# Layer 2 of a graph network with experts: both scores in one table row, experts' work rationed by columns, smaller last batches

## The chip, the cores and the metric

The kernel runs on one core of a Trainium2 chip. The metric is the device time of one execution in microseconds. Several executions are made, and the median counts. In the profile PE is TensorE (PEld are its weight loads), DVE is VectorE, ACT is ScalarE, POOL is GpSimd and SP is SyncE, which here only issues DMAs.

## The reference

The input has 6250 nodes of 256 features and 206,250 directed edges (src, dst). All is float32.

```python
def _gat_layer(x, src, dst, W, b, a, g, beta, N, concat):
    h = x @ W.T + b
    s_src, s_dst = h @ a[:d], h @ a[d:]
    e = jnp.exp(-leaky_relu(s_src[src] + s_dst[dst], 0.2))
    h_prime = segment_sum(e[:, None] * h[dst], src, num_segments=N)
    h_prime = (h_prime - mean) * rsqrt(var + 1e-5) * g + beta
    return elu(h_prime) if concat else h_prime
# layer 1: 8 heads of 64 features on layernorm(x), concatenated to 512
# layer 2: one head, 512 -> 256, elu;  x = x + that
# experts: t = layernorm(x); the 2 best of 8 by softmax(t @ router.T), weights normed to 1
#   y = t + sum over e of weight[e] * (gelu(t @ w1[e] + b1[e]) @ w2[e] + b2[e]);  x = x + y
```

## The kernel before

Nodes are cut into 49 blocks of 128 (the last has 106). One launch goes through three stages.

**The sort** (to about 440 us). The edges are sorted by the block of their src into slots of DRAM, on all engines. Beside it the table of layer 1 is made block by block: `products` (L357) multiplies the turned block by the weights, 512 features and 2x8 scores, `table_rows` (L366) copies them out of PSUM and stores a row of 520 numbers a node in `tab1`. `ph` is the bank of the features, `pk` that of the scores.

**Layer 1 and layer 2** are both run by `edges` (L587). A block has 34 tiles of 128 edges (the last 30), a group is up to 5 tiles (`GT`), so a block has 7 groups and a layer 342. A group goes through seven stages: `sources` loads the edges' places in the block (`rb`, SP); `gather` (L645) fetches the table row of each edge's dst, one indirect DMA a tile on POOL; `one_hot` (DVE) and `source_sums` (PE, `ps`) bring the src scores to the edges; `weigh` (DVE) adds the dst score from the row and ScalarE takes the Exp; `messages` (DVE) makes the weighted one-hot matrix `hot`; `add` (PE, L700) sums the messages into the block's PSUM bank `acc`. The order is written out by hand: a loop of ticks, in each of which every stage works on a group so many ticks ahead:

```python
stages = [(weigh, 2), (messages, 1), (source_sums, 4), (add, 0), (one_hot, 5), (sources, 5 + RB), (gather, GB)]
```

In layer 2 `GB` is 8, and there are as many gather buffers. Engines work in order, each through its own queue. A few "far" edges are added to every block at its end (`far_hot`).

When a block's last group is added, its `block_done` is put into `running`. It is a generator that is advanced once a tick, after the stages. In layer 1 (`middle`) it norms the block and multiplies it by layer 2's weights, and stores 257 numbers a node (256 features and the dst score) in `tab2` (L845), and the src score, one number a node, in `ssrc2` (L847). Layer 2 starts its gathers when the whole table is there.

In layer 2 (`tail`, L852) `block_done` (L902) norms the block, adds it to x (`xq`), norms again (`tok`), turns it on PE, multiplies by the router (`pl`) and, with the last block of a batch of `BB` = 4, finds the two best experts (`routes`). Then the batch's `experts` (L995) is put into `todo`, again a generator. Its steps are: `combine` (turn the weights, `pc`), 16 of `inner` (a half of one expert's first product for the whole batch, `ph`, L1019, then Gelu on ScalarE), `biases`, and 16 of `outer` (one expert's second product for two blocks, `py`, L1027, then two additions into `xq` on DVE, L1032). What takes a step's result off PSUM is issued two steps behind. After each tick `more` (L1069) issues steps:

```python
if steps is None:
    state["credit"] = min(state["credit"] + 1.5, 2.0)
    steps = int(state["credit"])
    state["credit"] -= steps
```

So a tick issues one or two steps, and after the last group all that is left is issued. There are 13 batches: twelve of four blocks and one of the last block alone. Where the sort's tables would overflow, another path through all edges (`every_edge`) is there; it is not taken with these inputs.

Of the kernel before, what the change touches and what calls it, by code (L numbers as in the profile page):

```python
# [31 lines left out]
P = 128  # L32
# [16 lines left out]
def kernel(ctx: ExitStack, tc: tile.TileContext, x, src, dst, w_heads, b_heads, a_heads,  # L49
# [8 lines left out]
    R2 = F + 1  # L58
# [34 lines left out]
    ssrc2 = dram.tile([NB * P, 1], F32, name="ssrc2")  # L93
# [263 lines left out]
    def products(b):  # L357
        ph = bank("ph", "ph")
        pk = bank("pk", "pk")
        for to, cols in ((ph, slice(0, HD)), (pk[:, :2 * H], slice(HD, C1))):  # L360
            for k in range(KF):
                nc.tensor.matmul(to, blocks[b][:, k, :], wt[:, k, cols], start=(k == 0), stop=False)
            nc.tensor.matmul(to, three, bias3[:, cols], start=False, stop=True)
        blocks[b] = ph, pk

    def table_rows(b):  # L366
        ph, pk = blocks.pop(b)
        row = sw.tile([P, C1], F32, name="row", bufs=2)
        nc.scalar.copy(row[:, HD:], pk[:, :2 * H])
        nc.scalar.copy(row[:, :HD], ph)  # L370
# [216 lines left out]
    def edges(es, layer, table, sel, ssrc, k, width, block_done, more=None):  # L587
# [3 lines left out]
        row = width + k  # L591
# [7 lines left out]
        groups = [(b, g) for b in range(NB) for g in range(-(-tiles[b] // GT))]  # L599
# [7 lines left out]
        def where(n):  # L607
            b, g = groups[n]
            return b, b // RBL, (b % RBL) * PITCH + g * GT

        def size(n):
            b, g = groups[n]
            return min(GT, tiles[b] - g * GT)
# [4 lines left out]
        def far_messages():  # L618
# [4 lines left out]
            ss = eb.tile([P, k], F32, name="far_ss")  # L623
            nc.gpsimd.indirect_dma_start(out=ss, out_offset=None, in_=ssrc,
# [7 lines left out]
            nc.vector.tensor_add(ss, ss, far_gt[:, width:])  # L632
# [6 lines left out]
        def sources(n):  # L639
            b, g = groups[n]  # L640
            r0 = b * PIT + g * GT * P
# [23 lines left out]
        def weigh(n):  # L665
# [4 lines left out]
            nc.vector.tensor_add(ssum, ssum, now[n]["gt"][:, :nt, width:])  # L670
# [6 lines left out]
        def messages(n):  # L677
# [17 lines left out]
            if n + 1 == len(groups) or groups[n + 1][0] > b:  # L695
# [4 lines left out]
        def add(n):  # L700
            b, g = groups[n]
# [11 lines left out]
        stages = [(weigh, 2), (messages, 1), (source_sums, 4), (add, 0), (one_hot, 5), (sources, 5 + RB), (gather, GB)]  # L713
        running = []
        t = -5 - RB
        with tc.manual_schedule():
# [5 lines left out]
            while t < len(groups) or running or (more and more(len(groups))):  # L722
# [9 lines left out]
                for of in list(running):  # L732
                    if of[0] <= t and next(of[1], True):
                        running.remove(of)
                if more and t < len(groups):
                    more()
                t += 1

    def every_edge(es, layer, table, ssrc, k, width):

        row = width + k
# [14 lines left out]
        with tc.For_i(0, EC, 1) as i:  # L756
# [7 lines left out]
            sg = gw.tile([EP, k], F32, name="sg")  # L764
            nc.gpsimd.indirect_dma_start(out=sg, out_offset=None, in_=ssrc,
                                         in_offset=bass.IndirectOffsetOnAxis(ap=si, axis=0))
            nc.vector.tensor_add(sg, sg, gt[:, width:])
# [34 lines left out]
    def middle(ms):  # L802
        mw = ms.enter_context(tc.tile_pool(name="mid_w", bufs=2))

        def block_done(b, acc):
# [39 lines left out]
            nc.sync.dma_start(tab2[b * P:(b + 1) * P, :], row[:, :R2])  # L845
# [315 lines left out]
```

## Time and profile before

| | |
|---|---|
| median of three executions | 5668.95 us (5641.82 to 5675.06) |
| profiled execution | 5686.65 us, span 5684.9, mean granted clock of TensorE 0.834 |
| busy | PE 4175.9 (73%), DVE 3288.7 (58%), POOL 3390.8 (60%), ACT 1309.7 (23%) |
| gathers L649 | 3324 on POOL, 965 ns each |

| stretch, us | PE busy | DVE busy | POOL busy | granted clock |
|---|---|---|---|---|
| 0 to 440, sort | 343.3 | 376.4 | 182.0 | 0.90 |
| 440 to 3110, layer 1 | 1944.0 | 1722.8 | 1596.9 | 0.82 |
| 3200 to 3450, layer 2, mostly without experts | 128.6 | 103.3 | 168.9 | 0.72 |
| 4000 to 4600, layer 2 with experts | 462.4 | 290.6 | 396.5 | 0.85 |
| 5585 to 5685, the end | 83.0 | 34.9 | 0.0 | 0.89 |

The views are read like this. The page's slices give each engine's busy share in 40 equal parts. A table of stretches gives busy time (and the number of instructions) of each engine between two moments. A row of the waits says who waited, for whom, how long in total, how often, and the longest. "issue" is idle time that no wait in the profile explains, "remote" one whose releaser is not told. The chain of waits goes back from the last instruction, at each step to what released it. A product in float32 appears as two rows of PE.

### The profile page before, as it was taken

How to read it: one execution, taken by the hardware profiler on the slowest of the kernel's cores; microseconds unless marked ns; L12 is line 12 of the kernel's file. 1: busy time of each engine (PE TensorE's matmuls, PEld its weight loads, DVE VectorE, ACT ScalarE, POOL GpSimd, SP SyncE). 2: the span in 40 equal slices, each digit the busy share in tenths (PEclk: the TensorE clock that was granted, in tenths of full speed). 3: DMA queues.
4: the chain of work that ended last, by engine and by line, in shares of the span. 5: the costliest groups of instructions: out<-in, count | busy, mean ns of one | idle time of the engine just before them, and what ended most of it. 6: DMA issues, size and time to landing. Idle time of an engine off the chain costs nothing.

```text
span 5684.9 us, 52631 instructions
## 1 busy us (share of the span) xinstructions
PE 4175.9 (73%) x16462; PEld 2477.2 (44%) x16462; DVE 3288.7 (58%) x8048; ACT 1309.7 (23%) x2440; POOL 3390.8 (60%) x3450
## 2 busy tenths in 40 slices
PE   5984777777777777777776447777778777777778
PEld 4762333333333333333333335555555555545556
DVE  9975666666666666666666334454444445444444
ACT  1220111111111111111111113333334333333433
POOL 3446656665666666666554666666666666666660
PEclk8996878888888888888778668888888888888989
DMA  2216767786677777777665544444444444444440
GB/s 69 66 51 186 196 187 188 195 210 182 195 192 186 201 190 194 190 195 191 184 189 141 141 118 111 122 119 113 119 122 112 121 120 120 113 119 122 112 112 14
DMA packets 378008, 825.33 MB, mean 145 GB/s; under 512 B 91759, under 2 KB 210779, under 8 KB 377718
## 3 DMA queue, kind: packets, MB, share of 16 engines
q0 software_dynamic: 216464, 665.03, 44.0%
q1 hardware_dynamic: 155868, 151.02, 9.5%
q10 hardware_dynamic: 5386, 5.83, 0.3%
q8 instruction: 131, 2.15, 0.2%
q14 instruction: 159, 1.30, 0.1%
HBM read 792.59 MB, written 28.99 MB: 145 GB/s over the span
## 4 chain that ended last, share of the span: by engine, by line
PE 35%; DVE 26%; issue 17%; another core or an unknown queue 12%; POOL 7%; DMA 2%; DVEq 0%; ACT 0%; POOLq 0%; ACTq 0%; SPq 0%
PE acc L705 18%; DVE msg L687 10%; POOL gt L649 7%; PE ph L1019 6%; PE py L1027 6%; DVE hot L684 2%; DMA gt<-tab,dst_idx 2%; DVE hot L693 1%; DVE ot L656 1%; PE run_ps L278 1%; PE ps L662 1%; DVE ssum L670 1%; DVE ssum L668 1%; DVE what L266 1%
## 5 line engine op out<-in xcount | busy, mean ns | idle before, releaser
L649 POOL DMA_INDIRECT gt<-tab,dst_idx x3324 | 3206.4, 965 | 1908.4 <-issue 923.3
L705 PE MATMUL acc<-msg,hot 128*128 128x512 f32 x3324 | 1711.6, 659 | 180.4 <-issue 178.6
L705 PE MATMUL acc<-gt,hot 128*128 128x256 f32 x3324 | 1004.0, 445 | 176.2 <-issue 167.8
L705 PEld LDWEIGHTS acc<-msg,hot 128*128 128x128 f32 x3324 | 666.4, 209 | 944.5 <-issue 942.9
L687 DVE TENSOR_TENSOR msg<-gt,ee 128x2560 f32<-128x2560 f32 (+1 forms) x342 | 935.2, 2735 | 0.0
L705 PEld LDWEIGHTS acc<-gt,hot 128*128 128x128 f32 x3324 | 697.7, 219 | 337.1 <-issue 230.5
L585 ACT ACTIVATE ee<-lr 128x40 f32<-128x40 f32 (+3 forms) x684 | 141.7, 207 | 2348.7 <-DVE lr L584 1250.0
L662 PE MATMUL ps<-sel,ot 128*128 128x24 bf16 (+1 forms) x3324 | 204.4, 171 | 649.7 <-issue 314.8
L693 DVE TENSOR_SCALAR hot<-iota_n,sloc,ee 128x128 f32<-128x128 f32 x1662 | 461.6, 357 | 330.9 <-remote 166.6
L684 DVE TENSOR_TENSOR hot<-iota_ps,sloc 128x640 f32<-128x640 f32 (+1 forms) x342 | 273.4, 799 | 603.8 <-remote 514.2
L662 PEld LDWEIGHTS <-ot 128*128 128x128 bf16 x3324 | 192.3, 100 | 945.5 <-issue 707.0
L1032 DVE SCALAR_TENSOR_TENSOR xq<-py,comb,xq 128x256 f32<-128x256 f32 x392 | 171.0, 478 | 577.2 <-remote 162.5
L1027 PE MATMUL py<-w2s,h 128*128 128x256 f32 x1568 | 410.5, 402 | 57.9 <-issue 52.9
L1019 PE MATMUL ph<-tokt,w1s 128*128 128x512 f32 (+1 forms) x832 | 408.0, 618 | 25.1 <-issue 23.6
L585 ACT ACT_TABLE_LOAD x252 | 323.3, 1283 | 375.8 <-DVE lr L584 178.6
L1027 PEld LDWEIGHTS py<-w2s,h 128*128 128x128 f32 x1568 | 312.2, 203 | 149.9 <-issue 99.9
L283 POOL DMA_INDIRECT srt<-run,to x92 | 168.4, 1830 | 247.9 <-DMA srt<-run,to 148.8
L668 DVE TENSOR_REDUCE ssum<-ps 128x40 f32<-128x120 f32 (+3 forms) x684 | 149.6, 219 | 252.8 <-remote 197.4
L656 DVE TENSOR_SCALAR ot<-rb,iota_p 128x640 bf16<-128x640 bf16 (+1 forms) x684 | 259.0, 379 | 7.2 <-DMA rb<-srow 7.2
L1019 PEld LDWEIGHTS ph<-tokt,w1s 128*128 128x128 f32 x832 | 162.4, 206 | 168.1 <-issue 157.9
L1021 ACT ACTIVATE h<-ph,b1s 128x512 f32<-128x512 f32 (+1 forms) x208 | 135.5, 662 | 368.1 <-remote 210.1
L840 PE MATMUL ph<-wo,ht 128*128 128x258 f32 x392 | 126.1, 476 | 84.8 <-DVE ht L837 79.1
(248 smaller groups left out, 3248.6 us busy)
## 6 DMA issues: line engine op xcount, KB each, us to landing
rb<-srow SPq DMA_DIRECT2D x588, 160.0 KB
gt<-tab,dst_idx POOLq DMA_INDIRECT x3324
tab<-row SPq DMA_DIRECT2D x49, 260.0 KB
rb<-srow SPq DMA_DIRECT2D x96, 128.0 KB
tab<-row SPq DMA_DIRECT2D x49, 128.5 KB
xq<-in_x_dram SPq DMA_DIRECT2D x12, 512.0 KB
out_dram<-xq SPq DMA_DIRECT2D x12, 512.0 KB
xc<-in_x_dram SPq DMA_DIRECT2D x6, 896.0 KB
```

Of the source, the lines that this page charges most:

```text
L585: nc.scalar.activation(ee, lr, AF.Exp, scale=-1.0)
L649: nc.gpsimd.indirect_dma_start(out=gt[:, j, :], out_offset=None, in_=table, in_offset=bass.IndirectOffsetOnAxis(ap=dst_idx[c][:, t0 + j:t0 ...
L656: nc.vector.tensor_scalar(ot[:, :cols], now[n]["rb"][:, :cols], iota_p, None, op0=OP.is_equal)
L662: nc.tensor.matmul(ps[:, j * 3 * k:(j + 1) * 3 * k], ot[:, j * P:(j + 1) * P], sel[:, groups[n][0]].rearrange("p t k -> p (t k)"), start=T ...
L668: nc.vector.tensor_reduce(ssum, now[n]["ps"][:, :nt * 3 * k].rearrange("p (j t k) -> p j k t", j=nt, t=3), axis=AX.X, op=OP.add)
L684: nc.vector.tensor_tensor(hot, iota_ps[:, None, :P].to_broadcast([P, nt, P]), sl[:, :, None].to_broadcast([P, nt, P]), op=OP.is_equal)
L687: nc.vector.tensor_mul(msg.rearrange("p j (h d) -> p j h d", h=k), gt[:, :, :width].rearrange("p j (h d) -> p j h d", h=k), ee[:, :, :, No ...
L693: nc.vector.tensor_scalar(hot[:, j, :], iota_n, sl[:, j:j + 1], ee[:, j, :], op0=OP.is_equal, op1=OP.mult)
L705: nc.tensor.matmul(accs[b][:, :width], now[n]["hot"][:, j, :], now[n]["msg"][:, j, :width], start=(g == 0 and j == 0), stop=False)
L1019: nc.tensor.matmul(ph[:, :W], w1s[:, e, k, f * P:(f + 1) * P], tokt[:, k, :W], start=(k == 0), stop=(k == KF - 1))
L1027: nc.tensor.matmul(py[:, (i - lo) * F:(i - lo + 1) * F], h1[:, k, i * P:(i + 1) * P], w2s[:, e, k, :], start=(k == 0), stop=(k == KF - 1))
L1032: nc.vector.scalar_tensor_tensor(xq[:, i, :], py[:, (i - lo) * F:(i - lo + 1) * F], comb[:, i, e:e + 1], xq[:, i, :], op0=OP.mult, op1=OP.add)
```

## The change

- **Both scores in layer 2's rows.** `tab2` has 258 numbers a node, the src score among them; `ssrc2` and its 49 stores are gone, and the one gather of far src scores reads whole rows.
- **Features in halves.** `products` makes 264 and 264 columns in the two banks in place of 512 and 16.
- **Order and groups.** Layer 2 begins with block 48 and then takes 0 to 47. In both layers the last group is cut in three: the last two parts have 2 tiles and 1.
- **Batches.** Sizes are 1 (block 48), 2, ten of 4, then 2, 2, 1, 1. Buffers of `xq` go from 4 to 6, those of `tokt`, `logits` and `comb` from 3 to 5.
- **Half steps.** In layer 2 `running` is advanced twice a tick: after `messages` and after all stages. `block_done` has two yields more.
- **Rationing.** Each step of the experts has a cost in columns (`inner` 2 x 128 x blocks, `outer` and `biases` by blocks), and `more` issues steps until a tick's columns are spent: 2048, in the last eight blocks' worth of ticks 3072, after the last group 6144. What is overspent is taken off the next tick.

```diff
-    R2 = F + 1
+    R2 = F + 2
...
-    ssrc2 = dram.tile([NB * P, 1], F32, name="ssrc2")
...
-        for to, cols in ((ph, slice(0, HD)), (pk[:, :2 * H], slice(HD, C1))):
+        for to, cols in ((ph[:, :C1 // 2], slice(0, C1 // 2)), (pk[:, :C1 // 2], slice(C1 // 2, C1))):
...
-        nc.scalar.copy(row[:, HD:], pk[:, :2 * H])
-        nc.scalar.copy(row[:, :HD], ph)
+        nc.scalar.copy(row[:, :C1 // 2], ph[:, :C1 // 2])
+        nc.scalar.copy(row[:, C1 // 2:], pk[:, :C1 // 2])
...
-        groups = [(b, g) for b in range(NB) for g in range(-(-tiles[b] // GT))]
+        order = list(range(NB)) if layer == 1 else [NB - 1, *range(NB - 1)]
+        groups = [(b, g, min(GT, tiles[b] - g)) for b in order for g in range(0, tiles[b], GT)]
+        b, g, n = groups.pop()
+        ends = [n - 3, 2, 1] if n > 3 else [n]
+        groups += [(b, g + sum(ends[:i]), end) for i, end in enumerate(ends)]
...
+        def step():
+            for of in list(running):
+                if of[0] <= t and next(of[1], True):
+                    running.remove(of)
...
                         if b is not None:
                             running.append((t + 2, block_done(b, accs.pop(b)[:, :width])))
-                for of in list(running):
-                    if of[0] <= t and next(of[1], True):
-                        running.remove(of)
-                if more and t < len(groups):
-                    more()
+                    if stage == messages and more:
+                        step()
+                step()
+                if more:
+                    more(2048 if t < len(groups) - 8 * -(-TILES // GT) else 3072 if t < len(groups) else 6144)
                 t += 1
...
-            nc.sync.dma_start(tab2[b * P:(b + 1) * P, :], row[:, :R2])
-            with nc.allow_non_contiguous_dma(reason="one element of a node"):
-                nc.sync.dma_start(ssrc2[b * P:(b + 1) * P, :], row[:, R2:])
-            nc.vector.tensor_copy(s2[:, b, :], row[:, R2:])
+            nc.sync.dma_start(tab2[b * P:(b + 1) * P, :], row)
+            nc.vector.tensor_copy(s2[:, b, :], row[:, F + 1:])
...
+        ends = [2, 2, 1, 1]
+        fours = (NB - 1 - sum(ends)) // BB
+        sizes = [NB - 1 - sum(ends) - fours * BB] + [BB] * fours + ends
+        sizes = [1] + [n for n in sizes if n]
+        firsts = [NB - 1] + [sum(sizes[1:i]) for i in range(1, len(sizes))]
...
             if i == 0:
-                while len(todo) > 1:
-                    more(1)
+                while len(todo) > 3:
+                    more(2048)
...
                 nc.tensor.transpose(pt[:, k * P:(k + 1) * P], tok[:, k * P:(k + 1) * P], ident)
             yield
             yield
+            yield
...
             yield
             yield
+            yield
             nc.vector.tensor_copy(logits[:, i, :], pl[:, :NE])
...
             def all_steps():
-                yield combine()
+
+                yield W, combine()
...
-                            yield inner(e, f, h1s[e])
+                            yield KF * W, inner(e, f, h1s[e])
...
-                            yield biases(lo, hi)
+                            yield (hi - lo) * F, biases(lo, hi)
                         else:
-                            yield outer(e - 1, lo, hi, h1s[e - 1])
+                            yield (hi - lo) * KF * F, outer(e - 1, lo, hi, h1s[e - 1])
...
-        def more(steps=None):
-
-            if steps is None:
-                state["credit"] = min(state["credit"] + 1.5, 2.0)
-                steps = int(state["credit"])
-                state["credit"] -= steps
+        def more(columns):
+
             some = bool(todo)
-            while todo and steps:
-                if next(todo[0], None):
-                    steps -= 1
+            state["credit"] = min(state["credit"], 0) + columns
+            while todo and state["credit"] > 0:
+                cost = next(todo[0], None)
+                if cost is None:
+                    todo.pop(0)
                 else:
-                    todo.pop(0)
+                    state["credit"] -= cost
             return some
```

## The prediction

> **What bounds the kernel now.** I read the page's slices first, then tables of stretches, then who waited for whom, then the chain of waits.
>
> ```profile
> PE   5984777777777777777776447777778777777778
> ...
> POOL 3446656665666666666554666666666666666660
> PEclk8996878888888888888778668888888888888989
> PE 35%; DVE 26%; issue 17%; another core or an unknown queue 12%; POOL 7%; DMA 2%; DVEq 0%; ACT 0%; POOLq 0%; ACTq 0%; SPq 0%
> ```
>
> Slices 1 to 3 are the sort (to about 440 us), then layer 1 (to 3110), then layer 2, then a stretch where only PE works. No engine fills its row. The chain names PE most, but it also holds much "issue" and "unknown", so stages must be asked one by one. Layer 2, where most of the change lies, first without experts, then with them, then at the end:
>
> ```profile
> core 0: us, PE busy (x) PEld busy (x) DVE busy (x) ACT busy (x) POOL busy (x), PEclk, DMA share, GB/s
> 3312.90:3426.20 113.30, 55.70 (x253) 39.83 (x252) 45.74 (x187) 18.54 (x36) 75.62 (x78) 0.70 0.44 118
> 3436.60:3606.90 170.30, 137.94 (x569) 94.34 (x568) 77.47 (x303) 63.96 (x88) 111.41 (x117) 0.87 0.44 112
> 3606.90:3634.90 28.00, 17.05 (x85) 12.85 (x83) 19.15 (x81) 7.01 (x12) 19.94 (x21) 0.88 0.60 162
> ```
>
> The last bracket counts gathers (L649). Without experts 78 take 113.3 us, 1.453 each; with them 117 take 170.3 us, 1.456 each. PE goes from 49% to 81% busy and the pace stays. In the five ticks after a batch (28 us) it is 1.333. So at 1.5 steps a tick PE is not what sets the pace. A gather itself takes 0.965 plus 0.30 of issue; the rest is waiting:
>
> ```profile
> POOL gt L649 <- issue: 366.1, 1201, 0.3
> POOL gt L649 <- remote: 108.4, 48, 3.6
> POOL gt L649 <- PE acc L705: 104.1, 53, 4.8
> ```
>
> That is 3500 to 5500 us. There 1363 gathers take 2000 us, 1.467 each: POOL's own 1686 us (1320 busy and 366 issue) and 310 of waits. `gather(n)` needs the buffer of group n-8, so POOL is held when PE's `add` is late. PE is late in spells in which it creeps without any wait shown:
>
> ```profile
> 3351.68 0.38 PE L705 MATMUL acc<-gt,hot 128*128 128x256 f32 x1 [0.22 <-issue]
> ...
> 3354.51 0.38 PE L705 MATMUL acc<-gt,hot 128*128 128x256 f32 x1 [1.20 <-issue]
> ```
>
> After the last gather there are no such spells, and PE is dense until the last block's reduction, then serial:
>
> ```profile
> 5549.60:5581.90 32.30, 32.30 (x148) 25.27 (x146) 15.00 (x55) 17.06 (x23) 0.00 (x0) 1.00 0.05 7
> 5581.90:5685.00 103.10, 85.05 (x338) 60.26 (x336) 37.48 (x123) 23.52 (x42) 0.00 (x0) 0.89 0.04 13
> ```
>
> In those 103 us the chain is the last block's chain (16 us), the rest of an old batch, a batch of four that begins with its combine transposes at 5602.8, and a batch of one:
>
> ```profile
> 5661.41 0.11 PE pc L1005
> ...
> 5677.22 0.48 DVE xq L1032
> ```
>
> A batch of four is 58.6 us, one of a single block 15.8, and storing takes the last 7.2.
>
> **The end of layer 2 (last batches of 2, 2, 1, 1).** Removed from behind the last gather are 58.6 and most of the old batch. By the program's order of instructions, ticks 335 to 343 now hold the last 34 tiles' adds, six groups of 5 and then small ones (2.6 us a full group, by 2.33 for ten passes plus 0.3 for `ps`), and up to 3072 columns of steps each, while any are left. A step of 1024 columns is 1.72 us (L1019 x4) to 1.73 (L1027 x8). Tick by tick that is 8.8, 6.8, 8.5, 6.6, 8.7, 4.0, 0.4, 5.3, 0.9: 50 us from the start of tick 335. POOL runs 5 to 6 groups ahead, so it issues the last gather about 9 us into this, leaving 41 (before: 32.3). After the last reduction comes two thirds of block 46's batch (10.5), then the last block's chain (16), then its batch (16.3, and 2 because PE has gone to half clock), then 7.7: 52.5. Sum 93.5 against 135.4: **-42**. Bounds -30 and -58 (POOL further behind or ahead).
>
> **Rationing by columns.** A batch of four costs 512 + 16x1024 + 2x512 + 16x1024 = 34,304 columns; at 2048 a tick that is 17 ticks with two steps and 11 of 28 with none, where now 25 ticks have 1.5. The total per 28 ticks is now 136 gathers x 1.467 = 199.5 us. The 11 empty ticks hold 53 gathers: 21 at 1.333 and 32 at 1.453, 74.5 us. The 83 gathers of the 17 full ticks are unknown; no stretch of the trace has two steps tick after tick. Lower bound: POOL's pace with steps, 1.456. Upper: PE becomes the path. Its 23 ticks in the second stretch are 7.3 us each with 1.4 of idle; half a step more is 0.87 / 0.87 = 1.0, so 8.3 a tick, 1.71 a gather, if none of the idle absorbs it. The lower row is nearer, since PE rose by 32 points of busy with no cost and two steps only bring it to some 94%, and since dense PE had clock 1.00. I take 1.49: 83 x 1.49 = 123.7, with 74.5 it is 198.2, **-1.3 to -1.5 a batch, about -16** over 10.5 to 12 batches' worth of ticks. Bounds: -55 and +165.
>
> The Trainium skill speaks against this bunching: its page "TensorE: Matmul & The Clock Gate", section "HAM oscillation — how this bites in real kernels", says that PE idle for a window of some 3.4 us falls to half clock and needs a busy window to return. The row agrees as far as clock goes: 0.70 without experts, 0.87 with. By the rule every batch then starts on a cold PE: 1.7 us more, +18 in all. By the row the pace was the same at 0.70, because adds of 4.6 us still fit in a tick of 7; gathers eight groups ahead cover the first cold steps. I take nothing.
>
> **More, smaller batches (16 in place of 13).** They add 3x32 L1019 products, 192 rows on PE; columns stay the same. The Trainium skill's page "Runtime: NRT & Kernel Launch", section "Instruction fetch mechanics", holds that streaming instructions is mostly hidden: 0. The trace has 299 us of "issue" idle before the acc, ps, py and ph products of 3500 to 5500, over 6437 products: 0.046 each, **+9**. I take the row. Three more loads and stores of xq stay on SP, 0.5 us each, behind which only `rb` loads wait that are six groups early: 0.
>
> **Half steps.** `step()` after `messages` advances a block twice a tick, and makes DVE wait: L896 now follows the Sqrt with only `one_hot` (0.38 us) between, where a table load is 1.28 and the Sqrt 0.20, so about 1.1 us, twice a block and once a batch for the Exp: 2.5 a block. Behind it queue `one_hot`, the experts' takes and the next `weigh`. DVE is busy 48% of 3500 to 5500, 26 us free in a block's 50: 0. Without that cover it is 49 x 2.5 = +120. The added yields keep PE's transposes and router products about as far ahead: 0.
>
> **Features in halves.** The sort from 250 to 403 us is PE end to end (151.2 of 153 busy):
>
> ```profile
> 277.33 1.72 PE ph L362 x4
> 279.06 0.22 PE ph L363
> 279.27 0.35 PE pk L362 x4
> ```
>
> With 0.02 for L363's second row a block costs 2.31 us. In halves of 264 columns eight passes are 8 x 0.43 x 264/512 = 1.77, the bias rows 0.23: 2.00. 25 blocks lie there: **-8**. Before 250 DVE is the fuller engine (185.7 of 190): 0. ScalarE's two copies (0.17 and 0.59) become two of about 0.38: the same. Bounds -4 and -14.
>
> **Both scores in a row, small last groups.** 49 stores of 4-byte elements leave SP (0.42 us of issue each, hidden everywhere but at layer 1's end), and rows of gathers grow from 1028 to 1032 bytes with DMA at 45%: 0. Between layers the first gather waits until 3114.8, 7.2 us after the last table store; the absent store is worth at most 1 of this. The last group of each layer in three parts lets its first adds start earlier but adds two rounds of small DVE operations (0.2 to 0.28 each); in layer 1 PE is dense from 3083 to the last add. **-2**; bounds -6 and +3. Block 48 first in layer 2 moves only which rows are fetched; all gathers wait for the whole table anyway.
>
> **Sum.** -42 - 16 + 9 - 8 - 2 = -59. The profiled execution took 5686.65 (span 5684.9), so 5628 on it; it lay 18 above the median of the runs shown (5668.95), and from that the forecast is **5610**.
>
> **Rivals.**
> 1. *Two steps a tick make PE the pacer.* Place: the 17 full ticks; price: 1.71 a gather gives 142 + 74.5 = 216.5, +17 a batch, +180 at most, against -43 for the rest: up to 5805. It decides from where the gain is eaten, +4 a batch, 1.55 a gather or 7.5 us a tick. For it: creeping spells are not absorbed by work, they add to it. Against: the equal pace of the two stretches. A mild form (1.60, +8 a batch) gives 5712.
> 2. *Rationing is neutral or eats half the gain*: 1.51 to 1.54, 5625 to 5660.
> 3. *Denser PE shortens the waits*: clock near 1.0 and POOL held less, the full ticks at 1.38: 115 + 74.5 = 189, -10 a batch, -110; with the rest 5515 to 5550. For it: 1.333 in the third stretch shows that POOL can go faster.
> 4. *The tail is moved, not shortened*: PE reaches tick 335 late, because steps no longer end before it. Half the gain goes: 5630.
>
> **How the numbers follow.** Forecast 0.50 (own range 5580 to 5635); rival 1 0.16; rivals 2 and 4 0.20; rival 3 0.14. The runs shown spread by 0.6%, so about 1% (57 us) is what can be told from no change: 5612 and 5726 are the edges. Rival 3 and two thirds of the forecast are faster: 0.47. Rivals 2 and 4 and the rest of the forecast are within: 0.37. Rival 1 is slower: 0.16. The range 5540 to 5705 leaves out the far halves of rivals 1 and 3.
>
> **What would show it.** Right: from the last gather's end to the end of the span under 100 us; L362 at about 2.0 us a block; 1.46 to 1.52 us a gather while two steps run and about 1.45 in empty ticks; granted clock higher in full ticks than in empty ones. Wrong: POOL's waits on PE acc well over 16% of layer 2, full ticks over 7.5 us, or L896 held by ACT with `weigh` late behind it.

## The result: 0.4% slower, and the profile after

The changed kernel took 5689.68 us (median; 5661.29 to 5708.85) beside 5664.6 us (5637.0 to 5689.52) for the kernel before: ratio 1.0044, 95% interval 1.0031 to 1.0057. The forecast was 5610, a gain of 59 us. The profiled execution took 5689.59 us with a span of 5687.8, so it is a middle one; that of before (5686.65) had been 22 above its median. The two profiles therefore differ by only 3 us, and most of the loss has to be found by pairs of runs.

Page of the changed kernel: busy tenths in 40 slices, and shares of the chain that ended last.

```profile
PE   5984777777777777777777465866876777687686
...
POOL 3446565566665656556554666666666666666661
PEclk9987888888888888888788687987987888898797
...
PE 31%; DVE 25%; issue 17%; another core or an unknown queue 14%; POOL 10%; DMA 2%; ACT 1%; DVEq 0%; POOLq 0%; ACTq 0%; SPq 0%
```

The bunching is seen at once: in layer 2 PE and its clock now go up and down. In layer 2 POOL's row is the same as before up to the end, where its last digit is 1 in place of 0: gathers run on for longer.

Stretches of layer 2 in the changed kernel (between two moments: busy time and count of instructions of each engine, granted clock, DMA): empty ticks, the first three ticks of a batch, full ticks; then two stretches with 3072 columns a tick, the second tick of a batch and then its full ticks.

```profile
core 0: us, PE busy (x) PEld busy (x) DVE busy (x) ACT busy (x) POOL busy (x), PEclk, DMA share, GB/s
3684.60:3754.60 70.00, 35.81 (x179) 26.44 (x177) 30.51 (x129) 10.27 (x22) 46.33 (x49) 0.76 0.47 123
3754.60:3790.00 35.40, 26.07 (x88) 15.69 (x86) 17.10 (x68) 14.56 (x19) 22.01 (x24) 0.76 0.45 123
3790.00:3857.20 67.20, 62.92 (x285) 44.89 (x281) 34.18 (x128) 37.75 (x46) 43.91 (x47) 0.97 0.45 116
5369.90:5388.90 19.00, 11.77 (x40) 6.78 (x39) 7.64 (x24) 10.54 (x13) 12.18 (x13) 0.82 0.40 104
5388.90:5457.60 68.70, 68.70 (x314) 50.77 (x313) 35.55 (x128) 36.78 (x46) 40.95 (x43) 1.00 0.41 103
```

The last bracket of busy times counts gathers. Full ticks: 47 in 67.2 us, 1.43 each, at clock 0.97. Empty ticks: 49 in 70.0, also 1.43. Between them lie three ticks that take 35.4 us together, in which PE has 88 rows where it has 285 in twice that time later. But POOL makes 24 gathers in them, 1.48 each: the ticks are long, the gathers hardly dearer. With 3072 columns PE is busy without a gap (68.70 of 68.70), and a gather takes 1.60. POOL's waits from 3500 to 5500 us are the same kind as before:

```profile
POOL gt L653 <- issue: 365.3, 1172, 4.4
POOL gt L653 <- PE acc L709: 126.8, 56, 5.5
POOL gt L653 <- remote: 70.6, 27, 3.6
```

Stage by stage, in us, from three pairs of profiles (the first is the pair of the record; the others, each on one chip, are r_before and r_after, r2_before and r2_after of the sets below; numbered gathers are those of layer 2; "tail" runs from the start of the last gather to the end of the span):

| stage | forecast | record | second pair | third pair |
|---|---|---|---|---|
| sort, to the first gather | -8 | 435.7 to 435.1 | 436.8 to 433.8 | 435.5 to 428.7 |
| layer 1's gathers | 0 | 2626.3 to 2639.7 | 2599.8 to 2622.9 | 2619.7 to 2657.6 |
| boundary to layer 2 | -2 | 52.7 to 46.7 | 50.3 to 47.6 | 59.3 to 47.6 |
| gathers 0 to 1360 | -7 (ration -16, batches +9) | 1989.7 to 1999.3 | 1972.5 to 1977.7 | 1990.2 to 1999.3 |
| gathers 1360 to 1661 | in the -7 | 444.1 to 456.5 | 435.3 to 471.2 | 440.6 to 458.2 |
| tail | -42 | 136.2 to 110.5 | 138.8 to 108.5 | 139.3 to 109.6 |

The tail gives 26 to 30 us. The last 301 gathers give back 12 to 36 of it, the other gathers of layer 2 5 to 10, and layer 1 13 to 38. Added up from its first gather to the end, layer 2 comes out even: -4, +11 and -3 us, where -49 was forecast; what makes the changed kernel longer than the kernel before in these pairs lies, for the most part, in layer 1. The second pair overstates the loss: the profile of the changed kernel is the slowest of its twelve executions, 26 us over their median.

### The profile page after: what moved, and what is told of

It is laid out like the page before. It is cut to its first block, busy times and chain, and to the rows that moved or that the text cites. A ratio compares the mean times of both kernels' runs of the same rounds, so it can differ in the third digit from the quotient of the medians.

```text
span 5687.8 us, 53177 instructions
## 1 busy us (share of the span) xinstructions
PE 4124.4 (73%) x16654; PEld 2504.4 (44%) x16654; DVE 3319.2 (58%) x8150; ACT 1411.3 (25%) x2559; POOL 3373.7 (59%) x3450
## 4 chain that ended last, share of the span: by engine, by line
PE 31%; DVE 25%; issue 17%; another core or an unknown queue 14%; POOL 10%; DMA 2%; ACT 1%; DVEq 0%; POOLq 0%; ACTq 0%; SPq 0%
PE acc L709 15%; POOL gt L653 10%; DVE msg L691 9%; PE ph L1036 6%; PE py L1044 5%; DVE hot L697 2%; DVE ot L660 2%; DVE hot L688 1%; DMA gt<-tab,dst_idx 1%; PE run_ps L277 1%; PE ps L666 1%; DVE what L265 1%; DVE ssum L674 1%; DVE ssum L672 1%
## 5 line engine op out<-in xcount | busy, mean ns | idle before, releaser
L709 PE MATMUL acc<-gt,hot 128*128 128x256 f32 x3324 | 981.8, 438 | 161.3 <-issue 141.1
L691 DVE TENSOR_TENSOR msg<-gt,ee 128x2560 f32<-128x2560 f32 (+2 forms) x344 | 935.5, 2720 | 0.0
L584 ACT ACTIVATE ee<-lr 128x40 f32<-128x40 f32 (+4 forms) x688 | 142.5, 207 | 2188.4 <-DVE lr L583 1042.5
L688 DVE TENSOR_TENSOR hot<-iota_ps,sloc 128x640 f32<-128x640 f32 (+2 forms) x344 | 273.7, 796 | 576.3 <-remote 420.8
L1036 PE MATMUL ph<-tokt,w1s 128*128 128x512 f32 (+2 forms) x1024 | 417.6, 543 | 17.8 <-DVE xq L1030 7.7
L1044 PE MATMUL py<-w2s,h 128*128 128x256 f32 x1568 | 381.9, 388 | 11.0 <-DVE xq L1030 7.0
L672 DVE TENSOR_REDUCE ssum<-ps 128x40 f32<-128x120 f32 (+4 forms) x688 | 150.2, 218 | 268.4 <-remote 226.6
L660 DVE TENSOR_SCALAR ot<-rb,iota_p 128x640 bf16<-128x640 bf16 (+2 forms) x688 | 266.5, 388 | 3.1 <-DMA rb<-srow 3.1
L1036 PEld LDWEIGHTS ph<-tokt,w1s 128*128 128x128 f32 x1024 | 200.7, 215 | 142.6 <-issue 107.8
```

What stands on the lines that cost most here:

```text
L584: nc.scalar.activation(ee, lr, AF.Exp, scale=-1.0)
L660: nc.vector.tensor_scalar(ot[:, :cols], now[n]["rb"][:, :cols], iota_p, None, op0=OP.is_equal)
L672: nc.vector.tensor_reduce(ssum, now[n]["ps"][:, :nt * 3 * k].rearrange("p (j t k) -> p j k t", j=nt, t=3), axis=AX.X, op=OP.add)
L688: nc.vector.tensor_tensor(hot, iota_ps[:, None, :P].to_broadcast([P, nt, P]), sl[:, :, None].to_broadcast([P, nt, P]), op=OP.is_equal)
L691: nc.vector.tensor_mul(msg.rearrange("p j (h d) -> p j h d", h=k), gt[:, :, :width].rearrange("p j (h d) -> p j h d", h=k), ee[:, :, :, No ...
L709: nc.tensor.matmul(accs[b][:, :width], now[n]["hot"][:, j, :], now[n]["msg"][:, j, :width], start=(g == 0 and j == 0), stop=False)
```

## The experiments

Five sets were run, each on one chip beside the kernel before. The kernel before took 5626.7 us in the first and 5626.9 in the second set, 4848.4 in the third, 5678.0 in the fourth and 5625.6 in the fifth, so only ratios and stages within a set are compared.

Three theories stood. **S**: at the start of a batch PE waits in order for DVE, adds stand behind it and gathers behind the adds. **B**: two steps a tick tire PE whatever the start. **H**: the half steps make DVE wait for ScalarE. Beside them **R**, that the longer rows cost something.

### First set: one part undone at a time

Even ration (u1_even):

```diff
-                    more(2048 if t < len(groups) - 8 * -(-TILES // GT) else 3072 if t < len(groups) else 6144)
+                    more(1536 if t < len(groups) - 8 * -(-TILES // GT) else 3072 if t < len(groups) else 6144)
```

> The changed kernel with 1536 columns a tick in place of 2048 (the late 3072 and 6144 stay), so that the steps of a batch of four are spread over 23 ticks and not bunched into 17. Theory S (batch starts: in the first two ticks of every batch all engines stand, 9 to 22 us a tick, whatever the ration): no change, 5680 to 5700, gathers of the middle (272nd to 1360th of layer 2) within 5 us of 1602. Theory B (bunching is the loss): the middle falls by 7 to 15 us to some 1590, time 5670 to 5680. Forecast's rival 3 (dense PE shortens waits): it would get slower, over 5700.

Whole steps (u2_whole):

```diff
-                    if stage == messages and more:
-                        step()
...
-            yield
```

(the last line three times: the added yields)

> The changed kernel with block_done advanced once a tick, after all stages, and without the three yields that were added: the half steps undone. Theory H (DVE's waits on ScalarE inside a tick, 70 us before the reciprocals of 3500 to 5500, hold one_hot and weigh, and the loss is there): the middle falls to about 1590 and the time to some 5670. Theories S and B, and the prediction's step (DVE has 26 us free in a block's 50): the middle stays within 5 us of 1602; the tail after the last gather gets longer by a few us since the last blocks' chains take more ticks: 5690 to 5700.

Batches of four to the end (u3_fours):

```diff
-        ends = [2, 2, 1, 1]
+        ends = []
```

> The changed kernel with block 48 alone and then twelve batches of four: no batches of 2, 2, 1, 1 at the end. Theory S (each batch start holds the gathers; two of the small batches start before the last gather and cost some 14 us there, last 301 gathers 456.5 where before had 444.1): the late stretch falls to about 445, and the tail grows from 110 to about 140 to 150 as before; sum 5700 to 5710. If the small batches are worth nothing in all (late loss and tail gain cancel): 5685 to 5695. By the prediction's sum (tail -42) it would be 5725 or more.

The rows alone, in the kernel before (a1_rows):

```diff
-    R2 = F + 1
+    R2 = F + 2
...
-    ssrc2 = dram.tile([NB * P, 1], F32, name="ssrc2")
...
-        edges(es, 2, tab2, sel2, ssrc2, 1, F, done, more)
+        edges(es, 2, tab2, sel2, tab2, 1, F, done, more)
```

> The kernel before with both scores in layer 2's row (1032 bytes a row) and nothing else. Prediction: 0 to -1. Theory R (longer rows slow layer 2's gathers, or the shifted tables slow layer 1, where the two profiles show 2639.7 after and 2626.3 before from the first to the last gather): +10 to +25 us, layer 1 near 2640 or layer 2's middle above 1600. If neither moves, layer 1's 13 us are scatter between executions: layer 1 anywhere in 2620 to 2640 over the four runs of this set, without order.

Measured: u1_even 0.9994 [0.998, 1.0009], u2_whole 0.9998 [0.9982, 1.0014], u3_fours 0.9999 [0.9985, 1.0014], a1_rows 1.0029 [1.0012, 1.0047]. Each of three different undos stood at the kernel before. The changed kernel itself was not run in this set; in the second it was at 1.003. That three parts should each carry the whole loss is odd, unless they share one place. The stages of u2_whole do not bear out H as it was put (middle 1586.1, no shorter than the others'), and S as it was put, that the ration doesn't matter to a start, failed with u1_even. The fours had two surprises. Their tail was the shortest, 98.8, not the 140 expected, so the small batches do not shorten it. And their last 301 gathers took 455.9 us, not the 445 expected (a1_rows: 436.0), so the small batches are not what makes that stretch long either.

### Second set: the yardsticks, and the rows undone

r_after is the changed kernel, r_before the kernel before, both as they are. u4_rows puts the src score back into its own column (the first two edits of a1_rows the other way round, and the gather and store that belong to them); m1_rows_even has the even ration besides.

> The changed kernel as it is, as the yardstick of this chip, and a second profile of it. If the loss is the same everywhere: ratio 1.004 to before, layer 1 some 13 us longer than before's. If layer 1's 13 us were scatter between executions, layer 1 lies within 8 us of before's here, and the ratio is then 1.000 to 1.004.

> The kernel before as it is: a second profile of it on the chip of the others (ratio 1.000). It tells how much a stage of one kernel moves between executions: by theory 'scatter' layer 1 moves by 10 us or more against 2626.3, the middle of layer 2 by up to 10 against 1595.4, the tail by less than 3 against 136.2.

> The changed kernel with the src scores back in ssrc2 (rows of 1028 bytes, 49 stores of one element a node more). The rows alone, put into the kernel before, had a ratio of 1.0029 [1.0012, 1.0047], some +16 us where the prediction had 0. Theory R: this kernel is 12 to 20 us faster than the changed one of this chip and no slower than before. Against R (the 16 us belong to how that kernel happened to lie, not to the rows): no difference to the changed kernel, within 5 us.

> The changed kernel with the src scores back in ssrc2 and 1536 columns a tick. If rows and bunching are two separate losses (R some 16 us, B some 20): ratio to before 0.993 to 0.996. If either undo alone brings all that is to be had: 0.999 to 1.000 as with the even ration alone (0.9994).

Measured: r_after 1.003 [1.0012, 1.0048], r_before 1.0017 [0.9998, 1.0036], u4_rows 1.0024 [1.0006, 1.0043], m1_rows_even 0.9983 [0.9965, 1.0]. The ratio of the loss is there again on a second chip, but the kernel before against itself shows what such a ratio can be off by: by medians r_after is only 4 us above r_before. The even ration takes 0.36 percentage points off (u1_even against r_after, two sets) and 0.41 with the rows undone (one set). The rows undone take off 0.06 and 0.11, within the scatter.

What do the helpful undos share? From the trace, the three ticks that begin with a batch's combine transposes (mean over the middle batches):

| kernel | three ticks, us | gathers in them | us a gather | batch starts before the last gather | ratio |
|---|---|---|---|---|---|
| r_before | 24.2 | 16.8 | 1.44 | 11 | 1.0017 |
| r_after | 37.2 | 24.7 | 1.51 | 14 | 1.0030 |
| u4_rows | 39.1 | 25.6 | 1.53 | 14 | 1.0024 |
| u3_fours | 38.5 | 24.9 | 1.55 | 12 | 0.9999 |
| u2_whole | 32.0 | 21.0 | 1.52 | 13 | 0.9998 |
| u1_even | 30.9 | 21.1 | 1.46 | 14 | 0.9994 |
| m1_rows_even | 30.3 | 20.9 | 1.45 | 14 | 0.9983 |

An undo either shortens the starts or makes fewer of them. But most of a start's length is not lost, since POOL goes on: three ordinary ticks hold 14.6 gathers, these hold 25, and POOL runs ahead while PE stands, until it has no buffer left. What a start costs is the price of its gathers, and that is lower only with the even ration. What whole steps gain is not explained by it, nor, but for their two starts fewer and their shorter tail, what the fours gain. This is one start of the profile of the record, in order of time (start, length, engine, line, what; in brackets the idle time before and its releaser), some POOL rows left out:

```profile
3759.44 0.19 DVE L1010 TENSOR_TENSOR comb<-one,one 128x32 f32<-128x32 f32 x1 [0.52 <-DVE one L1009]
...
3760.18 1.02 PE L1022 MATMUL pc<-ident,comb 128*8 128x128 f32 x4 [3.17 <-DVE comb L1010]
...
3761.00 4.62 PE L1036 MATMUL ph<-tokt,w1s 128*128 128x512 f32 x8
...
3766.47 0.95 POOL L653 DMA_INDIRECT gt<-tab,dst_idx  x1 [0.30 <-issue]
3770.19 0.68 DVE L1023 COPY ct<-pc 8x512 f32<-8x512 f32 x1 [10.55 <-remote]
3770.36 0.95 POOL L653 DMA_INDIRECT gt<-tab,dst_idx  x1 [2.94 <-remote]
3770.80 0.15 DVE L672 TENSOR_REDUCE ssum<-ps 128x5 f32<-128x15 f32 x1
...
3771.00 0.21 PEld L666 LDWEIGHTS <-ot 128*128 128x128 bf16 x5 [6.21 <-DVE ssum L672]
```

PE had finished the adds at 3757 and waits 3.17 us for `comb`, which DVE has just begun to make: `routes` ends and `more` issues the first steps in the same tick. It does the transposes and two steps' products, until 3765.6. DVE's copy `ct` needs the transposes, done by 3761.2, and starts at 3770.19; from 3765.6 on PE waits for `ssum`, which stands behind `ct` on DVE. POOL fills its last buffer at 3767.4 and stands too. Then all go on together. Why DVE starts so late the profile does not tell ("remote"). In the kernel before (record), adds came between the first steps of a batch: the first eight passes of `ph` took 8.1 us from first to last (median of eleven starts), in the changed kernel 4.6. That a late `ct` held less there is argued from this order, not measured.

### Third set: easing the start, and sizes

c1_start puts an empty step ahead of a batch and gives the transposes a whole tick:

```diff
-                yield W, combine()
+                yield 2048, lambda: None
+                yield 2048, combine()
```

c2_late has 1536 columns in every tick of the loop (two numbers of the line of u1_even). c3_even_fours joins u1_even and u3_fours. c4_order joins c2_late, u3_fours and u2_whole.

> The changed kernel with the start of each batch eased: the first step of a batch is left empty and the combine transposes get a tick's whole 2048 columns, so the first products come a tick after them, when ct has long been copied. Theory S (the loss is in the first three ticks of a batch, 37 us for 25 gathers in the changed kernel, 24.5 us before, since PE there waits in order for DVE's comb and ct and the next adds stand behind): three ticks from a batch's transposes fall to about 25 us, the middle from 1584 to about 1575 to 1580, the late stretch from 471 to about 455, the time to about 5620 (ratio 0.999). Theory B (two steps a tick tire PE whatever the start): no change in the time, 5635 to 5645, three ticks at 30 or more. The tail may lose some 5 us by empty steps.

> The changed kernel with 1536 columns in every tick up to the last group (the even ration had 3072 in the last 56 ticks). If the 3072 columns cause the slow late stretch (450.6 with them, 435 before): late falls to about 437, and the tail grows from 108 to some 125 to 130 since more is left; sum about the same as the even ration's 5617. If the small batches cause it: late stays at about 450.

> The changed kernel with 1536 columns a tick and batches of four to the end (3072 late). Both undos took off some 20 us each (ratios 0.9994 and 0.9999 to before, the changed kernel 1.0030). If they are separate losses (bunched starts in the middle, small batches in the late stretch): ratio 0.995 to 0.997, middle 1580, late 440 to 450, tail 99. If they are one: 0.999.

> The changed kernel with 1536 columns in every tick, batches of four, whole steps: of the change stay the order (block 48 first, so no batch of one at the end), the features in halves, both scores in a row and the small last groups. The prediction would have the lone last batch's 15.8 us and no more: tail about 120, ratio 0.997. By the twelve fours' tail of 98.8 with 3072 late, the tail is 100 to 120; late as before, 435 to 440; middle 1580: ratio 0.994 to 0.998.

Measured: c1_start 0.9822 [0.9808, 0.9835], c2_late 0.9828 [0.9815, 0.9842], c3_even_fours 0.9821 [0.9808, 0.9835], c4_order 0.9881 [0.9866, 0.9896]. On this chip the kernel before took 4848 us, 14% less than elsewhere, and the expectations don't fit: engines are not held. Page and POOL's waits (3115 to 4600 us) of c1_start:

```profile
PE   4994888888888888888885677897797788788797
...
POOL 2455777777777777777775777777777777777771
PEclk8997999999999999999997887998898898898898
```

```profile
POOL gt L653 <- issue: 297.6, 977, 0.3
POOL gt L653 <- PE acc L709: 25.0, 82, 0.3
```

No wait in these rows is over 0.3 us, and a gather takes 1.26 to 1.27, in full and in empty ticks alike. PE has no idle time called "issue" at all from 3115 us to the last gather; r2_before of the next set has 290 us of it before the `acc`, `ps`, `py` and `ph` products of 1900 us. In layer 2 POOL stood longer than about a microsecond twice, in the changed kernel of the record 152 times (before: 136). Here a batch's start costs nothing (23.2 us for 18.6 gathers, 1.25 each), and the last 301 gathers take 380 to 382 us in all four kernels, with 3072 columns or with 1536. Tails are 93.2, 97.7, 94.5 and, without 3072 columns, small batches and half steps, 118.9; that is most of the 30 us by which c4_order is behind c1_start. What c2_late was to tell, whether 3072 columns cause the long late stretch, it can't tell here: no kernel had fewer late columns where gathers are held. Of c1_start's 88 us only the tail can be placed, and that roughly, since there is no profile of the kernel before on this chip; the changed kernel was not run there.

### Fourth set: the start, where gathers are held

The same kernels once more: r2_before and r2_after, c1_start2 (c1_start), c3_even_fours2 (c3_even_fours).

> The kernel before as it is, for a profile on the chip of this set. If no engine creeps there (gathers at 1.25 to 1.28, some 4850 us): layer 1 near 2091, middle near 1380, tail some 130 to 137 and so the gain of the others lies in the tail and the boundary. If gathers are held: as before, 1580 in the middle and 435 late.

> The changed kernel as it is. Theory S with held handshakes: where gathers are held, 1.003 to 1.004 as on the two chips before; where they are not, batch starts cost nothing and the tail and boundary gain stays, some -60 to -90 us, ratio 0.980 to 0.988 with layer 2's gathers at 1.26. The prediction's own sum (-59) would be 0.988 there. If the loss belonged to the change's instruction count or its rows, the ratio would be above 1 on any chip.

> The changed kernel with the start of each batch eased (an empty step first, then the combine transposes with a tick's whole columns), the same kernel as in the run before. Where gathers are held: theory S 0.998 to 1.000 with the first three ticks of a batch at 25 to 30 us, theory B 1.003. Where they are not: the same as the changed kernel, within 5 us.

> The changed kernel with 1536 columns a tick and batches of four to the end, the same kernel as in the run before. Where gathers are held: 0.995 to 0.997 if the two losses are separate, 0.999 if one. Where they are not: within 5 us of the changed kernel, as four batches sizes and both rations gave 4760 to 4763 there.

Measured: r2_after 1.0027 [1.0005, 1.0048], c1_start2 0.9983 [0.9962, 1.0003], c3_even_fours2 0.9975 [0.9952, 0.9998]; r2_before is a single execution (5686.48 us). Easing the start alone takes 30 us off the median (5702.39 to 5672.53), with two steps a tick as before. B had no change here and S had 0.998 to 1.000, so B, as it was put, falls and S stands, though the two intervals nearly touch. The profiles differ by 39 us. Layer 1, on which the edit has no hold, makes 15 of them (2657.6 to 2642.4), so the edit's own part is some 26: gathers 0 to 1360 went from 1999.3 to 1991.0, the last 301 from 458.2 to 451.0 and the tail from 109.6 to 99.6. Three ticks at a start went from 37.4 us (1.52 a gather) to 31.0 (1.47). c3_even_fours2 is between "separate losses" and "one". PE's waits from 3500 to 5400 us (who waited for whom: us in all, times, longest), r2_before:

```profile
PE ps L662 <- issue: 117.1, 69, 5.5
PE acc L705 <- issue: 101.3, 122, 2.5
PE py L1027 <- issue: 56.0, 79, 2.3
PE ps L662 <- DVE ssum L668: 30.8, 13, 7.7
PE pc L1005 <- DVE ssum L668: 24.4, 4, 7.2
```

r2_after:

```profile
PE ps L666 <- DVE ssum L672: 145.1, 35, 11.7
PE acc L709 <- issue: 124.1, 139, 3.3
PE ps L666 <- issue: 51.0, 25, 10.4
PE pb L1028 <- DVE xq L1030: 46.6, 7, 8.8
PE pc L1022 <- DVE comb L1010: 25.5, 8, 8.4
```

c1_start2:

```profile
PE acc L709 <- issue: 159.5, 183, 3.3
PE ps L666 <- DVE ssum L672: 81.6, 34, 7.4
PE ps L666 <- issue: 62.7, 25, 8.9
PE pt L950 <- DVE tok L912: 40.8, 8, 9.0
```

The waits that the change brought are those for DVE: 145 us for `ssum` where it was 55 in two rows, 47 for `xq` behind `pb`, 26 for `comb` where it was 11. With the start eased the last two are gone from the top rows and the first is nearly halved; 41 us for `tok` are new.

### Fifth set: what helped, together, and the rows once more

d1_all is u4_rows with the edits of u1_even, u3_fours and c1_start; a1_rows2 is a1_rows again.

> The changed kernel with batch starts eased, 1536 columns a tick, batches of four to the end, and the src scores in their own column (rows of 1028 bytes). If rows cost layer 1 some 10 to 30 us and the starts 25: ratio 0.990 to 0.995, layer 1 shorter than that of the rows alone in this set by 7 to 30 us, its packets at 245 ns. If layer 1 only scatters: 0.995 to 0.998.

> The kernel before with both scores in a row and nothing else, the same kernel as before. Rows cost layer 1: ratio 1.002 to 1.006 and layer 1 longer than the other kernel's of this set. Rows cost nothing: 0.999 to 1.001.

Measured: d1_all 0.9973 [0.9957, 0.999], a1_rows2 1.0014 [1.0002, 1.0026]. d1_all is 0.3% faster than the kernel before, no more than just beyond what that kernel shows against itself (1.0017). Its starts are down to 24.8 us, its tail is 103.3. Its ratio is the one expected if layer 1 only scatters, though its layer 1 is 13 us shorter than that of a1_rows2. Its last 301 gathers still take 454.8, with 3072 columns a tick and no small batches; a1_rows2 has 436.6. a1_rows2 itself lies between the two ranges given for it.

For the rows, layer 1 speaks mostly in one direction. In each set that has both forms, it is longer with both scores in a row: 2639.7 against 2626.3 in the record; 2622.9 against 2599.8, 2603.7 and 2604.8 in the second set; 2657.6, 2642.4 and 2657.7 against 2619.7 in the fourth; 2612.5 against 2599.1 in the fifth. In the first set, which has rows only, it was 2598.4 to 2609.7, as short as the others' without. Layer 1's code is the same in the three changed kernels of the fourth set, and their times spread by 15 us, and the rows undone in the changed kernel gained only the 0.06 and 0.11 points above. So a cost of some 10 to 30 us is likely, but not proven, and why it should be there is open. Its gathers' packets of 4160 bytes took 244 to 247 ns on the mean with the column and 222 to 226 without, so they moved faster and layer 1 did not get shorter. Instructions of PE, DVE, ACT and POOL stand in the same order in layer 1 but for its last group; SP's do not, as its 49 stores are gone.

## Why the prediction failed, point by point

In the three pairs of profiles the sum came to +3, +28 and +16 us where it had -59. The gathers of layer 2 took +22, +41 and +27 in place of -7, layer 1 +13, +23 and +38 in place of 0, the tail -26, -30 and -30 in place of -42. Four steps failed: the start of a batch was taken at nothing, the last 301 gathers were priced like the rest, two ticks of the tail were priced by passes alone, and layer 1 was given nothing.

**Rationing (forecast -16).** Over eight whole batches (28 ticks each) a batch went from 200.4 to 201.2 us in the record, 198.0 to 199.0 and 200.0 to 201.4 in the other pairs, where 199.5 to 198.2 was forecast. The prices were nearly right: in the record full ticks, the starts among them, took 1.50 a gather (forecast 1.49) and empty ones 1.43 (74.5/53 = 1.41). Clock, too, went as forecast: 0.97 in full, 0.76 in empty ticks. But 1.3 us a batch was the small difference of two large sums, and what was left out is as large. The step that failed is "gathers eight groups ahead cover the first cold steps. I take nothing." The start of a batch was looked at for clock alone. Its handshakes, `comb` to `pc` to `ct` to `pb` to `xq` between DVE and PE, were not in the sum at all, though the trace of before had the waits of PE for them. They are in every batch. Three ticks became 13 us longer. In most of that time POOL made 8 gathers more, which the forecast had put into the empty ticks, where a gather is cheaper. By price, the first three ticks took 1.53, 1.50 and 1.52 a gather and the other full ones 1.49, 1.45 and 1.48: 0.9 to 1.4 us a start. In c1_start2 the difference is gone (1.47 and 1.49), and the gathers of layer 2 gained 16 us over 14 starts.

From the rule that I set aside (the Trainium skill, "TensorE: Matmul & The Clock Gate", section "HAM oscillation — how this bites in real kernels"), that PE idle for some 3.4 us falls to half clock, I had estimated 1.7 us a batch. The first eight passes took 4.6 where two warm steps take 2 x 1.72 = 3.44, so 1.2: the cold start is there, and as large as the loss. But it is not what the change brought: in c1_start2 these passes take 4.6 as well (mean of the batches of four), and before, the first four took 3.1, 2.4 and 2.9 us in the three profiles, where a warm step takes 1.72.

Rival 1 named PE as the pacer, and the full ticks as the place. Full ticks took 8.0 us, beyond the 7.5 it asked, but with 5.4 gathers in each: the place was wrong. Its sign was right. Two bounds of this term do not follow from its figures: +17 a batch gives +180 to +200, not +165, and 1.456 for full ticks gives -44 to -50, not -55.

**The tail (forecast -42, measured -26).** From the last gather's end to the last reduction the forecast had 41 us, and it took 61; what follows had 52.5 and took 49. The failed terms are tick 335, "8.8", which took 21.7, and tick 342, "5.3", which took 15.7. PE there:

```profile
5564.64 2.41 PE L709 MATMUL acc<-gt,hot 128*128 128x256 f32 x10
5570.91 0.38 PE L1022 MATMUL pc<-ident,comb 128*8 128x128 f32 x2 [3.87 <-DVE comb L1010]
5571.14 2.66 PE L1036 MATMUL ph<-tokt,w1s 128*128 128x256 f32 x8
5577.62 2.07 PE L1028 MATMUL pb<-b2s,ct 8*128 8x256 f32 x4 [3.82 <-DVE ct L1023]
...
5628.36 0.38 PE L1022 MATMUL pc<-ident,comb 128*8 128x128 f32 x1 [4.71 <-DVE comb L1010]
```

Both are a batch's start: two waits of 3.8 us in the first, and the gathers had not even ended; one of 4.7 in the second, and then 9.8 us of PE until the last adds, for steps that were priced at 5.3. The forecast counted passes and no handshake.

The last 301 gathers took 12 to 36 us more, and the forecast priced them like the rest. The small batches are not the reason: without them the stretch took 455.9, 452.3 and 454.8 (u3_fours, c3_even_fours2, d1_all). All kernels with 3072 columns there took 450 to 471 where gathers are held, those of before, with 1.5 steps a tick, 435 to 444; full ticks in it took 1.52 to 1.61 a gather against 1.45 to 1.49. With 3072 columns a tick takes 7.5 to 8 us of unbroken PE, 1.60 a gather in the stretch above: rival 1's mechanism, only in the last eight blocks. This is argued, since no run had fewer columns there with gathers held; easing the starts alone took 7 us off. The forecast had used 3072 columns in the tail's sum without asking what they do to POOL before it. So rival 4 (the tail is moved, not shortened) came nearest: the last 301 gathers and the tail together changed by -13, +6 and -12 us.

**More batches (+9).** Sized by unexplained idle time before PE's instructions. That time fell: before the `acc`, `ps`, `py` and `ph` products of 3500 to 5400 it was 290 us in r2_before and 183 in r2_after, while waits for DVE rose. What the added batches cost by themselves was not measured; the reason given for +9 is wrong.

**Half steps (0).** The size was right: 70 us of DVE's waits before the reciprocal L911 from 3500 to 5500, for some 100 forecast. Whether "26 us free in a block's 50" hid all of it is open. Without half steps a start is 5 us shorter (37.2 to 32.0) but holds 4 gathers less, 1.52 each against 1.51, and the middle of layer 2 was no shorter. The undo brought 0.3 points between two sets, with intervals that just touch.

**Features in halves (-8, measured -0.6 in the record, -3.0 and -6.8 in the other pairs).** The products did get shorter as forecast, 1.05 + 0.28 and again 1.05 + 0.28, overlapping to 2.02 a block:

```profile
277.30 1.05 PE L361 MATMUL ph<-wt,xt 128*128 128x264 f32 x4
278.19 0.28 PE L362 MATMUL ph<-bias,three 65*128 65x264 bf16 x1
278.31 1.05 PE L361 MATMUL pk<-wt,xt 128*128 128x264 f32 x4
279.20 0.28 PE L362 MATMUL pk<-bias,three 65*128 65x264 bf16 x1
```

The last block's features were done 7.5 us earlier (their last pass began at 388.4, where it was 395.9). But the sort ends with POOL's scatters to `srt`, one after another at some 2.45 us. In the record they were 3.8 us ahead at 391 us; then one waited 6.2 us for DVE (L499), and the last began at 426.0, before at 426.4. "PE end to end" was true and not the bound of the end. In the third pair nearly all of the forecast came, so this is not so in every execution.

**Scores in a row and small groups (-2).** The boundary gained 3 to 12 us. It was 52.8 and 47.4 with the rows alone, 50.3 in r_before, and 46.7 to 50.4 in the kernels with small groups of the same sets: which of the two parts gives it is not settled. Layer 1 had been given nothing ("49 stores of 4-byte elements leave SP", rows 4 bytes longer: 0), and moved by the +13 to +38 above. In two of the three pairs that is the largest loss of any row of the table above, and its cause stays open.

## What to carry to other kernels

When work is bunched, price its first ticks by themselves: list the handshakes between engines at the start, and what stands behind each on an engine that works in order. Price a long tick by what the slowest stream gets done in it, not by its length. A gain at the end that is won by starting more things before the end must be charged to the stage before; sum both. And if one kernel gains 1.8% on one chip and less than 0.3% on another, the mechanism to look for is the one that is absent on the first.

## What the runs showed of the hardware that was not expected

- In four of the five sets, and in the runs of the record, engines were held while gathers flowed; in the third set they were not. Over all of layer 2 a gather took 1.45 to 1.48 us where they were held and 1.26 to 1.27 where they were not. In layer 1 the packets took the same time (222 ns at 4160 bytes for r_after and c1_start), and its gathers 2622.9 and 2092.1 us. The whole program is 14% shorter. What makes the difference isn't in the profile; it is open. That it is the chip is not shown: the fourth and the fifth set ran on one chip, with 5678 and 5626 us for the kernel before.
- Where they are held, more than half of DVE's long stands end as POOL goes on. In layer 2 of the record's profile of before DVE had some 155 stands of over 3 us; 87 of them ended within 0.6 us of the moment at which POOL went on after one of its own, where chance would give 7%. In the changed kernel it was 75 of 164, in c1_start none of 141. In the start shown above, a result of PE that was there by 3761.2 is used by DVE at 3770.19 and the buffer freed at 3757 by POOL at 3770.36. Whether a signal is late or an instruction, the profile does not tell.
- With the src score's column gone, the packets of layer 1's gathers took 224 ns on the mean in place of 246. The median is 161 ns in both; what shrank is the slowest hundredth (from some 1500 to 830 ns). Layer 1 also has 6600 packets of 4 bytes fewer then. Whether these stores or the place of the tables did it was not tried.
